# A four-layer convolutional sequence on one core: layer 1's edges reordered, layer 3's preparation with full-width products and a split in two parts

## The chip, the cores and the metric

The kernel runs on one core of a Trainium2 chip. A core has TensorE (PE, matrix products into the accumulator memory PSUM), VectorE (DVE), ScalarE (ACT), GpSimd (POOL) and SyncE (SP, which here only issues transfers). Each engine has an instruction queue of its own, worked through in order; transfers (DMAs) are issued from such a queue and run beside it. The metric is the time of one launch on the device in microseconds (us).

## The reference

Four layers on x of shape (4, 128, 64, 64), float32. In the kernel an image is a tile of 128 partitions (channels) by N = 4096 pixels. The change touches layers 1 and 3.

Layer 0 is an attention with 1x1 products. Layer 1 applies twice a 3x3 convolution with weights rounded to powers of two, and after it an "adder" convolution, then batch norm:

```python
def per_channel(wc):
    return -jnp.sum(jnp.abs(p - wc[None, :, None]), axis=1)
...
out = adder_conv(shift_conv(x, w_shift1, stride=1), w_add1)
out = jax.nn.relu(batchnorm(out, bn1_gamma, bn1_beta))
out = adder_conv(shift_conv(out, w_shift2, stride=1), w_add2)
out = batchnorm(out, bn2_gamma, bn2_beta)
return jax.nn.relu(out + residual)
```

Here p are the 3x3 patches: for each of 128 output channels and each pixel, 1152 absolute differences are summed. The batch norm takes mean and variance over all four images. Layer 2 is an attention with an MLP. Layer 3 splits x by two small maps, projects, and runs a selective scan forwards and backwards over the 4096 pixels:

```python
m = jax.nn.sigmoid(jnp.einsum('bchw,oc->bohw', cat, illum_w[:, :, 0, 0]) + illum_b[None, :, None, None])
f_low = x * m
f_high = x * (1.0 + alpha * curr_grad)
hidden = _rms_norm(seq, rms_w)
xz = jnp.einsum('blc,ec->bel', hidden, in_proj_w)
xs, z = jnp.split(xz, 2, axis=1)
xs = _causal_conv1d(xs, conv_w[:, 0, :], conv_b)
...
delta = jax.nn.softplus(jnp.einsum('brl,dr->bdl', dt, dt_proj_w) + dt_proj_b[None, :, None])
...
return f_mamba + gamma * f_low
```

seq is f_high with its pixels in a row, cat is x with the illumination map as a 129th channel, and both maps have one value per pixel for all channels.

## The kernel before

The program is one pass over the layers; between layers images lie in DRAM (x1d, y1d, y2d) or, in layers 2 and 3, in four image tiles in SBUF (xp[0] to xp[3]). Most instructions are written through a helper that keeps the written order on each engine, so the order of the text is the order of each queue.

**Layer 1.** `layer1` (L535) loads and rounds the weights of both convolutions first: `quantized` (L282) loads one set (L287) and `quantize` (L259) rounds it in nine DVE operations; this is done for both before anything else. `shift_adder` (L292) is then called once for each adder, with the prefix a1 or a2 in the tiles' names. At its start it loads the adder's weights wa (L306), makes negated columns wn (L311) for ACT's biases and a masked copy w_third (L327 to L329), and computes wsum, the sums of wa over input channels, with 192 small matmuls (L335) into the PSUM tile pw, copied at L339. Then it convolves image 0: `fetch` loads rows of the input with a border (xin), nine matmuls (L375) for each of eight blocks of 512 pixels fill a PSUM bank, and DVE copies it into the padded image pb (L380).

The main part walks over 512 units (4 images x 128 output channels). A unit is built from several 128x4096 tiles: absolute values on ACT (L456), maxima on DVE (L470), one of both (L462), and the tiles of `pair` (L474): for each half of the image two maxima on DVE (L479), which a POOL DMA adds into one tile (L481). Each tile is summed over channels by matmuls with a `pick` of 31 zero columns and one non-zero (L425) into PSUM. The order of these steps is written out by hand in a table (ORDER, L43 to L48), for four units at a time; its entries C take three steps of the generator `beside` (L404), which holds the sums of the present image's patches (L387 to L402) and the convolution of the next image. After every 32 units `evacuate` (L432) adds the sums and writes a chunk: L437 and bn_stats L440 on DVE, then the stores to y_d (L442). The four chunks of an image are 32 output channels each.

`batchnorm_scale` (L541) stores all statistics to DRAM (stats_d, L543), reads them back with the channels in the partitions (byco, four DMAs, L546), aggregates them (L550), and takes Ln, Exp and a product (L553) for the scale. The second adder's convolution normalizes its input as it fetches it (`normed`, L571 to L575). After the second adder, `residual` of layer 2 (L660) loads x<-y2d (L671) and applies the scale (L673, L676, L677).

**Layer 3.** `layer3_prepare` (L1004) runs its images one after the other. PSUM has eight banks of 128x512 here, all with the tag mm. The steps:

- `split(b)` (L1042): for each of eight blocks of 512 pixels it loads a row of both maps (mr, L1051), multiplies x by the illumination weights (pm, L1053), adds the illumination row by a product with one row (L1054), and spreads the gradient row by another product with one row (pg, L1056). ACT takes the sigmoid (sg, L1058); DVE makes f_high (fh, L1059) and gamma·f_low (L1061), which is stored (low_d, L1062).
- `norm(b)` (L1064): the RMS norm of fh: squares on ACT, the mean by a product (pv, L1074), Ln and Exp, the scaling on DVE (L1081).
- `project(b)` (L1084): in four pieces of 2048 pixels: px (L1099) copied by ACT (pre, L1100), a causal convolution of four DVE operations per piece (L1122, L1124), pz (L1106) with Silu on ACT (sz, L1108) and its store (L1109), Silu of the convolved piece (xs, L1127) and its store (L1129).
- `steps_of(b)` (L1131): pxd (L1143), copied by DVE (xd, L1146), pd (L1155), dv (L1158), and the softplus over ee and uu on DVE and ACT (L1160 to L1175), a POOL product (L1177), with stores of 1024 columns (delta_d, du_d).

The loop at L1196 runs split(0), norm(0); then for each image project(b), split(b+1), and steps_of(b) with norm(b+1) beside it, one step of norm for two of steps_of. `layer3_scan` (L1215) follows; it reads low_d back and adds a bias in an Identity activation (L1455).

Of the kernel before, what the change touches and what calls it, by code (L numbers as in the profile page):

```python
# [9 lines left out]
F32 = mybir.dt.float32  # L10
# [251 lines left out]
def quantize(nc, sb, w, of, name):  # L262

    flat = [P, TAPS * P]
    aw = sb.tile(flat, F32, tag="qa", name=f"{name}_aw")
    nc.vector.tensor_scalar(aw.bitcast(I32), w.bitcast(I32), 0x7FFFFFFF, None, ALU.bitwise_and)

    pw = sb.tile(flat, F32, tag="qp", name=f"{name}_pw")
    nc.vector.tensor_scalar(pw.bitcast(I32), w.bitcast(I32), 0x7F800000, None, ALU.bitwise_and)
    up = sb.tile(flat, F32, tag="qu", name=f"{name}_up")  # L270
    nc.vector.scalar_tensor_tensor(up, pw, 1.4142135381698608, aw, ALU.mult, ALU.is_lt)
    nc.vector.scalar_tensor_tensor(pw, up, 1.0, pw, ALU.add, ALU.mult)
    nc.vector.scalar_tensor_tensor(pw, aw, 0.005, pw, ALU.is_ge, ALU.mult)
    sg = sb.tile(flat, I32, tag="qu", name=f"{name}_sg")
    nc.vector.tensor_scalar(sg, w.bitcast(I32), -0x80000000, None, ALU.bitwise_and)
    nc.vector.tensor_tensor(pw.bitcast(I32), pw.bitcast(I32), sg, ALU.bitwise_or)
    nc.vector.tensor_tensor(pw, pw, w, ALU.subtract)
    nc.vector.tensor_tensor(of, w, pw, ALU.add)


def quantized(tc, pool, w_shift, tag):

    nc = tc.nc
    wqs = pool.tile([P, TAPS, P], F32, name=f"{tag}wq")
    with tc.tile_pool(name=f"{tag}q", bufs=1) as qp:
        ws = qp.tile([P, TAPS * P], F32, name=f"{tag}ws")
        nc.sync.dma_start(ws, w_shift)  # L287
        quantize(nc, qp, ws, wqs.rearrange("p t o -> p (t o)"), tag)
    return wqs


def shift_adder(tc, cm, load, wqs, w_add, stats, y_d, tag):  # L292
# [10 lines left out]
    with ExitStack() as ctx:  # L303
        cp = ctx.enter_context(tc.tile_pool(name=f"{tag}c", bufs=1))
        wa = cp.tile([P, TAPS, P], F32, name=f"{tag}wa")
        nc.sync.dma_start(wa.rearrange("p t o -> p (t o)"), w_add)  # L306
        wn = {}
        for t, scale in [(t, 1.0) for t in ABS_TAPS[0]] + [(ABS_TAPS[c][i], 0.5) for c, i in HALF.items()]:
            if (t, scale) not in wn:
                wn[t, scale] = cp.tile([P, P], F32, name=f"{tag}wn{t}_{len(wn)}")  # L310
                nc.vector.tensor_scalar(wn[t, scale], wa[:, t, :], -scale, None, ALU.mult)  # L311

        pick = {}
        for v in (-1.0, -2.0):
            pick[v] = cp.tile([P, 63], F32, name=f"{tag}pick{int(-v)}")
            nc.vector.memset(pick[v], 0.0)
            nc.vector.memset(pick[v][:, 31:32], v)
        third = cp.tile([P, 32], F32, name=f"{tag}third")
        nc.vector.memset(third, 0.0)
        nc.vector.memset(third[:, 2:32:4], 1.0)  # L320
# [5 lines left out]
        with tc.tile_pool(name=f"{tag}w", bufs=1) as wt:  # L326
            w_third = wt.tile([P, P], F32, name=f"{tag}wthird")  # L327
            nc.vector.memset(w_third, 0.0)
            nc.vector.tensor_copy(w_third[:, 2:P:4], wa[:, MAX_TAPS[3], 2:P:4])  # L329
            pw = ps_c.tile([P, NC], F32, tag="cv", name=f"{tag}pw")  # L330
            for c in range(NC):
                for g in range(4):
                    for i, t in enumerate(sum_taps):
                        w = w_third if t == MAX_TAPS[3] else wa[:, t, :]
                        nc.tensor.matmul(  # L335
                            pw[32 * g : 32 * g + 32, c : c + 1], w[:, 32 * c : 32 * c + 32], cm.one_col,
                            start=(i == 0), stop=(i == len(sum_taps) - 1), skip_group_check=True,
                        )
            nc.vector.tensor_copy(wsum, pw)  # L339
# [64 lines left out]
        def beside(b, pb_of):  # L404

            yield from sums_of_p(b, pb_of[b], sp_of[b])
            if b < B - 1:
# [4 lines left out]
        for _ in convolution(0, pb_of[0]):  # L412
            pass
# [19 lines left out]
        def evacuate(chunk):  # L433
            b, c = divmod(chunk, NC)
            for k in range(2):
# [6 lines left out]
                nc.sync.dma_start(to[k], o)  # L442

# [29 lines left out]
        def pair(n, h):  # L473
# [7 lines left out]
            then(nc.gpsimd.dma_start(ms[1], ms[0], accum_op=ALU.add))  # L481
# [53 lines left out]
def layer1(ctx, tc, cm, w_shift1, w_add1, g1, b1, w_shift2, w_add2, g2, b2, x1d, y1d, y2d, stats_d):  # L535
# [5 lines left out]
    def batchnorm_scale(stats, at, gamma, name):  # L541

        nc.sync.dma_start(at, stats.rearrange("p c s v -> p c (s v)"))  # L543
        byco = lp.tile([P, 4, 2 * B * 6], F32, name=f"byco{name}")
        for c in range(4):
            nc.sync.dma_start(  # L546
                byco[32 * c : 32 * c + 32], at[:, c, :].rearrange("(g j) s -> j g s", g=4)
            )
# [11 lines left out]
    wq1, wq2 = quantized(tc, lp, w_shift1, "a1"), quantized(tc, lp, w_shift2, "a2")  # L560
# [6 lines left out]
    shift_adder(tc, cm, plain, wq1, w_add1, stats1, y1d, "a1")  # L567
    mean1, sc1 = batchnorm_scale(stats1, stats_d[0], vec["g1"], "1")
# [11 lines left out]
    shift_adder(tc, cm, normed, wq2, w_add2, stats2, y2d, "a2")  # L580
    mean2, sc2 = batchnorm_scale(stats2, stats_d[1], vec["g2"], "2")
# [422 lines left out]
def layer3_prepare(  # L1004
    tc, cm, xp, maps_d, illum_w, illum_wl, illum_b, rms_w, in_w, conv_w, conv_b, x_w, dt_w, dt_b,
    alpha, gamma, low_d, xs_d, sz_d, delta_d, du_d, xdbl_d,
# [3 lines left out]
    with ExitStack() as ctx:  # L1010
# [14 lines left out]
        ga = load([P, 1], gamma.partition_broadcast(P), "ga")  # L1025
# [4 lines left out]
        xw = load([P, 2, NX], x_w, "xw")  # L1030
        dtw = load([DT_RANK, 2 * P], dt_w, "dtw")
# [3 lines left out]
        iwr = cp.tile([1, P], F32, name="iwr")  # L1035
        nc.vector.tensor_scalar(iwr, cm.ones[0:1, :], iwl, None, ALU.mult)
        alr = cp.tile([1, P], F32, name="alr")
        nc.vector.tensor_scalar(alr, cm.ones[0:1, :], al, None, ALU.mult)
# [3 lines left out]
        def split(b):  # L1042

            fh = big.tile([P, N], F32, tag="fh", name=f"fh{b}")
            fh_of[b] = fh
            for k in range(NB):
                u = f"{b}_{k}"
                c = bass.ts(k, BK)
                src = inner(xp, b, k)
                mr = sb.tile([1, 2, BK], F32, tag="mr", name=f"mr{u}")  # L1050
                nc.sync.dma_start(mr, maps_d[:, b, c].rearrange("(o i) n -> o i n", o=1))  # L1051
                pm = ps.tile([P, BK], F32, tag="mm", name=f"pm3_{u}")
                then(nc.tensor.matmul(pm, iwm, src, start=True, stop=False))  # L1053
                then(nc.tensor.matmul(pm, iwr, mr[:, 0, :], start=False, stop=True))  # L1054
                pg = ps.tile([P, BK], F32, tag="mm", name=f"pg{u}")
                then(nc.tensor.matmul(pg, alr, mr[:, 1, :], start=True, stop=True))  # L1056
                sg = sb.tile([P, BK], F32, tag="sg", name=f"sg{u}")
                then(nc.scalar.activation(sg, pm, AF.Sigmoid, bias=ib))  # L1058
                then(nc.vector.scalar_tensor_tensor(rows(fh[:, c]), rows(pg), 1.0, src, ALU.add, ALU.mult))  # L1059
                yield  # L1060
                then(nc.vector.scalar_tensor_tensor(rows(sg), src, ga, rows(sg), ALU.mult, ALU.mult))  # L1061
# [653 lines left out]
```

## Time and profile before

| what | us |
|---|---|
| median of three runs (lowest to highest) | 21133.91 (21114.99 to 21178.35) |
| the profiled execution's own time | 21155.93 |
| its span | 21154.1 |
| PE busy | 19660.1 |
| DVE busy | 18970.2 |
| ACT busy | 17550.0 |
| POOL busy | 7577.3 |

By stage, in the profiled execution (us from the start of the span):

| stretch | what |
|---|---|
| 0 to 1980 | layer 0 |
| 1980 to 2090 | layer 1's weights and the first convolution of image 0 |
| 2090 to 9400 | first adder |
| 9400 to 9504 | its end, statistics, and image 0's second convolution |
| 9504 to 16850 | second adder |
| 16850 to 17880 | its end, and layer 2 |
| 17880 to about 18540 | layer 3's preparation |
| about 18540 to 21154 | layer 3's scan |

Busy times are sums of instruction durations on an engine. A chain of waits is followed back from the last instruction to what released each step, so its pieces lie one after the other in time; a piece named DMA is the time from a transfer's issue to its landing. A float32 matmul of 512 columns appears as two records. The granted PE clock is a share of the full clock.

### The profile page before, as it was taken

What the parts mean: (1) busy time and instruction counts of PE and PEld (TensorE: products, weight loads), DVE (VectorE), ACT (ScalarE), POOL (GpSimd) and SP (SyncE); (2) the same over time, 40 slices, a digit from 0 to 9 for tenths busy, and PEclk for the clock granted to TensorE, in tenths of its full rate; (3) what the DMA queues carried; (4) which work ended last, traced back from release to release, by engine and by line L of the source; (5) the groups of instructions that cost most, each with busy time, mean ns of one, the idle gap of its engine ahead of it and who ended that gap; (6) DMA issues with size and microseconds to landing.
All of it is one profiled execution on the core that took longest, in us unless ns stands there. A gap on an engine that the chain in (4) does not pass through costs nothing.

```text
span 21154.1 us, 323001 instructions
## 1 busy us (share of the span) xinstructions
PE 19660.1 (93%) x139180; PEld 6292.0 (30%) x139180; DVE 18970.2 (90%) x12273; ACT 17550.0 (83%) x9055; POOL 7577.3 (36%) x3844
## 2 busy tenths in 40 slices
PE   9998999999999999999999999999999877789998
PEld 4443222222222222222222222222222223223333
DVE  7876999999999999989999999999999887799998
ACT  5664999999999999989999999999999833466666
POOL 5665222222222222212222222222222100189998
PEclk9999999999999999999999999999999988699999
DMA  0000777777777777767777777777777710389997
GB/s 13 9 9 20 147 152 148 147 154 149 151 145 152 150 143 151 156 136 145 150 148 152 149 148 151 147 149 147 147 154 153 162 21 20 130 238 251 253 253 218
DMA packets 576191, 2970.17 MB, mean 140 GB/s; under 512 B 164572, under 2 KB 165476, under 8 KB 240804
## 3 DMA queue, kind: packets, MB, share of 16 engines
q0 software_dynamic: 296800, 2160.20, 51.0%
q1 hardware_dynamic: 277812, 787.19, 13.0%
q8 instruction: 1089, 17.84, 0.3%
q14 instruction: 346, 2.83, 0.0%
q10 hardware_dynamic: 144, 2.10, 0.0%
HBM read 662.03 MB, written 128.78 MB: 37 GB/s over the span
## 4 chain that ended last, share of the span: by engine, by line
PE 43%; issue 15%; DMA 14%; DVE 14%; ACT 11%; POOL 3%; SPq 1%; DVEq 0%; POOLq 0%; ACTq 0%
PE a1pa L425 15%; PE a2pa L425 13%; DMA ma<-ma 10%; ACT aa L456 9%; PE pe L164 4%; PE pav L207 4%; DVE h L1364 4%; DVE ma L479 3%; DVE da L470 2%; DMA du<-du_d 2%; DVE g L854 1%; POOL ma L481 1%; PE mg L1379 1%; DMA dl<-delta_d 1%; PE a1pc L375 1%
## 5 line engine op out<-in xcount | busy, mean ns | idle before, releaser
L481 POOL DMA_DIRECT2D ma<-ma x2048 | 3799.7, 1870 | 10892.9 <-DVE ma L479 7671.8
L456 ACT ACTIVATE aa<-a1pb,a1wn 128x4096 f32<-128x4096 f32 x1920 | 6959.4, 3711 | 485.5 <-PE a1pa L425 342.0
L456 ACT ACTIVATE aa<-a2pb,a2wn 128x4096 f32<-128x4096 f32 x1920 | 6964.9, 3712 | 358.9 <-PE a2pa L425 340.4
L425 PE MATMUL a1pa<-aa,a1pick 128*32 128x512 f32 x30720 | 3616.8, 600 | 84.4 <-ACT aa L456 81.3
L425 PE MATMUL a2pa<-aa,a2pick 128*32 128x512 f32 x30720 | 3617.2, 600 | 82.6 <-ACT aa L456 81.3
L470 DVE TENSOR_SCALAR da<-a2pb,a2wa 128x4096 f32<-128x4096 f32 x1408 | 3271.0, 2350 | 316.1 <-PE a2pa L425 316.1
L470 DVE TENSOR_SCALAR da<-a1pb,a1wa 128x4096 f32<-128x4096 f32 x1408 | 3269.6, 2350 | 306.8 <-PE a1pa L425 306.5
L425 PE MATMUL a1pa<-da,a1pick 128*32 128x512 f32 x22528 | 2696.1, 597 | 15.2 <-DVE da L470 15.2
L425 PE MATMUL a2pa<-da,a2pick 128*32 128x512 f32 x22528 | 2680.8, 594 | 18.0 <-DVE da L470 18.0
L479 DVE TENSOR_SCALAR ma<-a1pb,a1wa 128x2048 f32<-128x2048 f32 x2048 | 2529.8, 1282 | 71.1 <-DMA ma<-ma 71.1
L479 DVE TENSOR_SCALAR ma<-a2pb,a2wa 128x2048 f32<-128x2048 f32 x2048 | 2530.6, 1282 | 63.5 <-DMA ma<-ma 63.3
L1379 PE MATMUL mg<-h,ident 128*128 128x512 f32 x4096 | 1955.8, 615 | 214.6 <-ACT m L1388 174.0
L1364 DVE TENSOR_TENSOR_SCAN h<-da,h,dbu 128x1024 f32<-128x1024 f32 x768 | 1804.3, 2349 | 126.1 <-ACT da L1350 32.2
L425 PEld LDWEIGHTS a1pa<-aa,a1pick 128*32 128x32 f32 x30720 | 982.4, 111 | 2492.5 <-issue 2130.5
L425 PEld LDWEIGHTS a2pa<-aa,a2pick 128*32 128x32 f32 x30720 | 983.1, 111 | 2488.0 <-issue 2132.9
L425 PE MATMUL a2pa<-ma,a2pick 128*32 128x512 f32 x8192 | 1094.2, 607 | 266.0 <-DMA ma<-ma 265.8
L425 PE MATMUL a1pa<-ma,a1pick 128*32 128x512 f32 x8192 | 1096.2, 608 | 239.1 <-DMA ma<-ma 239.1
L201 POOL TENSOR_TENSOR ssum<-ssum,et 128x512 f32<-128x512 f32 x960 | 1230.0, 1281 | 233.0 <-ACT et L196 166.1
L425 PEld LDWEIGHTS a1pa<-da,a1pick 128*32 128x32 f32 x22528 | 716.9, 110 | 1747.2 <-issue 1612.4
L425 PEld LDWEIGHTS a2pa<-da,a2pick 128*32 128x32 f32 x22528 | 714.8, 110 | 1739.7 <-issue 1584.1
L462 DVE SCALAR_TENSOR_TENSOR aa<-a2pb,a2wa,aa 128x4096 f32<-128x4096 f32 x256 | 1147.4, 4482 | 81.8 <-ACT aa L456 81.7
L462 DVE SCALAR_TENSOR_TENSOR aa<-a1pb,a1wa,aa 128x4096 f32<-128x4096 f32 x256 | 1147.4, 4482 | 78.2 <-ACT aa L456 78.0
(295 smaller groups left out, 17707.1 us busy)
## 6 DMA issues: line engine op xcount, KB each, us to landing
ma<-ma POOLq DMA_DIRECT2D x2048, 1024.0 KB, 8.9
dl<-delta_d SPq DMA_DIRECT2D x256, 512.0 KB
dl<-delta_d SPq DMA_DIRECT2D x512, 256.0 KB
du<-du_d SPq DMA_DIRECT2D x256, 512.0 KB
du<-du_d SPq DMA_DIRECT2D x512, 256.0 KB
sz_d<-sz SPq DMA_DIRECT2D x64, 256.0 KB
xs_d<-xs SPq DMA_DIRECT2D x8, 2048.0 KB
delta_d<-dv SPq DMA_DIRECT2D x32, 512.0 KB
```

Of the source, the lines that this page charges most:

```text
L164: nc.tensor.matmul(pe, k[:, bass.ts(j, P)], unit[u, "q"], start=True, stop=True)
L201: nc.gpsimd.tensor_tensor(unit[u, "sum"], unit[u, "sum"], at, ALU.add)
L207: nc.tensor.matmul(unit[u, "av"], image[u // NB][2][:, j, :], at, start=(j == 0), stop=(j == NJ - 1))
L375: then(nc.tensor.matmul(pc, wqs[:, t, :], here[:, y : y + RB, x : x + W], start=(t == 0), stop=(t == TAPS - 1),))
L425: then(nc.tensor.matmul(pa[k][32 * g : 32 * g + 32, :], pick[v][:, 31 - jj : 63 - jj], d[:, bass.ts(4 * at + g, BK)], start=(n // 32, k) n ...
L456: then(nc.scalar.activation(rows(at), view(n, t), AF.Abs, bias=bias, scale=scale))
L462: then(nc.vector.scalar_tensor_tensor(rows(at), view(n, ADDED_TAP), weight(n, ADDED_TAP), rows(at), ALU.max, ALU.add))
L470: then(nc.vector.tensor_scalar(rows(dt), view(n, t), weight(n, t), None, ALU.max))
L479: then(nc.vector.tensor_scalar(rows(mt), v, weight(n, t), None, ALU.max))
L481: then(nc.gpsimd.dma_start(ms[1], ms[0], accum_op=ALU.add))
L1364: then(nc.vector.tensor_tensor_scan(t[:, cols][:, s], da[:, s], st[n, "dbu", h][:, cols][:, s], 0.0 if e % 4 == 0 else st["last"], ALU.mul ...
L1379: then(nc.tensor.matmul(pm, cm.ident, st[n, way, h][:, bass.ts(k, BK)], start=(way == 0), stop=(way == 1)))
```

## The change

In layer 1:

- Only the first convolution's weights are rounded before it. The second's are loaded behind the first input rows, and their nine DVE operations stand between the copies of image 0's convolution, as do wn and w_third; wa's load is moved there too. The rounding's temporaries take tiles of the maxima's tag "am".
- The 192 small matmuls for wsum become eight further steps of `beside` for image 0, after the sums of patches and ahead of image 1's convolution.
- The memsets of pick and third go from DVE to POOL.
- For the last unit, `pair` issues no accumulating DMA: both maxima are summed by matmuls of their own.
- Statistics don't go through DRAM: at each evacuation of the last image, four DMAs copy the chunk's statistics from SBUF to byco in SBUF; in the last chunk two of them are issued on ACT's queue.

In layer 3:

- The one-row and eight-row operands (map rows, iwr, alr, dtw) and the 40-column one (xw) are padded with zeros to 128, so that each product is 128 by 128. Each map row is loaded by a DMA of its own into the first row of a padded tile, two tiles for each map.
- `split` is divided. `high(b)` has the pg products and fh; for b ≥ 1, fh is written into the buffer of xp[b-1]. `low(b)` has the pm products into eight PSUM banks, eight sigmoids into tiles of the tags dv, ee and uu, four POOL products of 1024 columns, and four stores.
- high(b+1) runs beside project(b), two steps per piece; low(b+1) follows at its end. For image 0 the order is high, norm, low.
- The factor gamma is no longer in f_low; the scan's Identity activation applies it as its scale.

In the compiled order, some small ACT and DVE operations for the scan's constants also stand earlier, in the last image's projection and steps, with four more loads of ACT's function tables.

The diff, cut to its core:

```diff
-def quantized(tc, pool, w_shift, tag):
...
+def quantize(tc, pool, w_shift, of, name):
+    w, aw, pw, up = [
+        pool.tile([P, HL], F32, tag="am", name=f"{name}_q{k}")[:, 0 : TAPS * P] for k in range(4)
+    ]
+    nc.sync.dma_start(w, w_shift)
+    yield
...
-            nc.vector.memset(pick[v], 0.0)
-            nc.vector.memset(pick[v][:, 31:32], v)
+            nc.gpsimd.memset(pick[v], 0.0)
+            nc.gpsimd.memset(pick[v][:, 31:32], v)
...
             yield from sums_of_p(b, pb_of[b], sp_of[b])
+            if b == 0:
+                yield from sums_of_w(w_third)
             if b < B - 1:
...
-        for _ in convolution(0, pb_of[0]):
-            pass
+        quantizing = [quantize(tc, mp, w, of, f"{tag}{k}") for k, (w, of) in enumerate(shifts)]
+        for q in quantizing[:1]:
+            for _ in q:
+                pass
+        for at, _ in enumerate(convolution(0, pb_of[0])):
+            if at == 0:
+                nc.sync.dma_start(wa.rearrange("p t o -> p (t o)"), w_add)
+                for q in quantizing[1:]:
+                    next(q)
+            if at % TAPS == 4 and at > 2 * TAPS:
+                for q in quantizing[1:]:
+                    next(q, None)
+            if at == 2 * TAPS + 1:
+                negated()
...
+            if b == B - 1:
+                for g in range(4):
+                    (nc.scalar if c == NC - 1 and g % 2 else nc.sync).dma_start(
+                        byco[32 * c : 32 * c + 32, g, :],
+                        stats[32 * g : 32 * g + 32, c, :, :].rearrange("p s v -> p (s v)"),
+                    )
...
-            then(nc.gpsimd.dma_start(ms[1], ms[0], accum_op=ALU.add))
+            if n < B * P - 1:
+                then(nc.gpsimd.dma_start(ms[1], ms[0], accum_op=ALU.add))
+            else:
+                streams[n, "q", h] = (-2.0, ms[0], (h,))
             streams[n, "p", h] = (-2.0, ms[1], (h,))
...
-        nc.sync.dma_start(at, stats.rearrange("p c s v -> p c (s v)"))
-        byco = lp.tile([P, 4, 2 * B * 6], F32, name=f"byco{name}")
-        for c in range(4):
-            nc.sync.dma_start(
-                byco[32 * c : 32 * c + 32], at[:, c, :].rearrange("(g j) s -> j g s", g=4)
-            )
...
+        map_rows = [[padded([P, BK], f"map{i}_{j}") for j in range(2)] for i in range(2)]
+        def map_row(i, b, k):
+            t = map_rows[i][k % 2]
+            nc.sync.dma_start(t[0:1, :], maps_d[i, b, bass.ts(k, BK)].rearrange("(o n) -> o n", o=1))
+            return t
...
-        def split(b):
+        def low(b):
+            halves = []
+            for k in range(NB):
+                pm = ps.tile([P, BK], F32, tag="mm", name=f"pm3_{b}_{k}")
+                then(nc.tensor.matmul(pm, iwm, inner(xp, b, k), start=True, stop=False))
+                then(nc.tensor.matmul(pm, iwr, map_row(0, b, k), start=False, stop=True))
+                halves.append(pm)
+            yield
+            for k2, tag in enumerate(("dv", "ee", "uu", "dv")):
+                sg = sb.tile([P, 2 * BK], F32, tag=tag, bufs=3, name=f"sg{b}_{k2}")
+                for i in range(2):
+                    then(nc.scalar.activation(sg[:, bass.ts(i, BK)], halves[2 * k2 + i], AF.Sigmoid, bias=ib))
+                src = xp[b][:, 2 * RB * k2 : 2 * RB * (k2 + 1), :].rearrange("p h w -> p (h w)")
+                then(nc.gpsimd.tensor_tensor(sg, src, sg, ALU.mult))
+                nc.sync.dma_start(low_d[b, :, bass.ts(k2, 2 * BK)], sg)
+        def high(b):
+            if b == 0:
+                fh = big.tile([P, N], F32, tag="fh", name="fh0")
+            else:
+                fh = xp[b - 1].rearrange("p h w -> p (h w)")
...
+                pg = ps.tile([P, BK], F32, tag="mm", name=f"pg{b}_{k}")
+                then(nc.tensor.matmul(pg, alr, map_row(1, b, k), start=True, stop=True))
                 yield
...
                 if i + 1 < len(pieces):
                     projected(*pieces[i + 1])
+                next(beside, None)
+                next(beside, None)
...
+                if i + 1 == len(pieces):
+                    next(beside, None)
+                    next(behind, None)
                 then(nc.scalar.activation(xc, xc, AF.Silu, bias=cb[:, mc : mc + 1]))
...
+            next(behind, None)
...
-            project(b)
-            if b < B - 1:
-                for _ in split(b + 1):
-                    pass
+            more = b < B - 1
+            project(b, high(b + 1) if more else iter(()), low(b + 1) if more else iter(()))
...
-            then(nc.scalar.activation(fl, fl, AF.Identity, bias=lb))
+            then(nc.scalar.activation(fl, fl, AF.Identity, scale=ga, bias=lb))
```

## The prediction, before the result was known

> **What bounds the kernel now.** I read the page's 40 slices first, then busy time by stage, then the chain of waits at each stage's edge. By stage (columns: stretch, its length, busy PE, weight loads, DVE, ACT, POOL, granted PE clock, DMA share, GB/s):
>
> ```profile
> 1980.00:2090.00 110.00, 72.69 (x336) 35.88 (x336) 27.18 (x42) 0.00 (x0) 1.50 (x12) 0.77 0.19 48
> 2090.00:9400.00 7310.00, 6978.05 (x62196) 2043.13 (x62200) 6852.77 (x3804) 6960.73 (x1921) 1874.26 (x1059) 0.98 0.74 150
> 17886.00:17932.00 46.00, 45.63 (x48) 13.30 (x48) 10.18 (x17) 7.63 (x10) 0.00 (x0) 0.50 0.15 48
> 17947.00:17974.00 27.00, 27.00 (x65) 11.93 (x64) 23.93 (x17) 20.40 (x32) 0.00 (x0) 1.00 0.32 126
> ```
>
> Layer 1's two main stretches hold 94 to 95% on PE, ACT and DVE at once, 14,660 us in all: no step added there is quite free. What the change can shorten lies between them. Edge A is 110 us in which ACT does nothing. The third row is one image's split in layer 3: PE is full, but at half clock (0.50); the projection beside it (fourth row) runs at 1.00.
>
> The chain at edge A (start, length, what):
>
> ```profile
> 1980.56 3.76 DMA a1ws<-in_w_shift
> ...
> 1994.89 3.60 DMA a2ws<-in_w_shift
> ...
> 2009.07 3.66 DMA a1wa<-in_w_add
> 2012.76 0.91 DVE a1wn L311 x6
> ...
> 2013.82 7.17 PE a1pw L335 x182
> 2021.00 3.77 DMA a1xin<-x1d
> ```
>
> Between the end of the first quantizing (1994.89) and the first convolution product (2025.02) lie 30.1 us of serial work that this convolution doesn't use. After the first adder and after the second:
>
> ```profile
> 9406.08 7.09 DMA ma<-ma
> ...
> 9417.28 7.26 DMA a2wa<-in_w_add
> ```
>
> ```profile
> 16841.48 7.04 DMA ma<-ma
> ...
> 16852.18 11.66 DMA stats_d<-stats
> ```
>
> In both the last unit's accumulating DMA is 7 us with nothing beside it. Then the statistics travel through DRAM: after the second, 11.66 us before SP may issue the reads, and the first x load of layer 2 stands behind them on SP (issued 16869.77, used 16878.51).
>
> [...]the split is busy 45.63 of 46 us and still at 0.50. Of its three products a block two have one row of 128 (L1054, L1056)[...].[...] The smallest load here takes 2.1 us (iw, 17883.90 to 17885.98).[...] Here DVE L1168 takes 3.25 us (at 18092.58) beside a POOL product, 1.23 without.
>
> **Layer 1, part by part.** Edge A: the second quantizing (3.60 + 10.5), wa's load (3.66), six wn and the third (1.0), the 192 small products (8.0) and the last load (3.8) leave the path. The second quantizing and wn move to DVE inside the first convolution, where PE has 64.9 us and DVE 8 copies of 0.7: they hide; uncovered they would be 11.5 us. Both moved loads, w_shift2 and wa, queue on SP behind the three xin loads already issued, so the convolution's start isn't held. Start about 1995.5 in place of 2025.0: −29.5. The small products run in the main stretch of image 0: 8 us where PE has 5% free; bounds 0 and +8 (an addition can't gain), I take +4. They also push the next image's convolution by 8 of the 93 steps of 3 products, which still ends before the image does. Edge A: −25.
>
> Edge B: the last unit's two maxima go straight to PE, 16 more matmul records; the pairs' 8 records took 1.97 cold, so +1 to +2 for −7.1: statistics ready about 8.3 sooner (9408.5). They go SBUF to SBUF, each chunk's four pieces at its own evacuation, so three quarters are sent long before. The last four DMAs are split over SP and ACT (0.4 each); landing isn't in this trace: bounds 2.1 (iw) and 7.3 (wa, under load); I take 2.5, byco there at about 9411. In before bn_aggr started at 9426.16 and the convolution 12.3 later, held mostly by PE's small products (9424.65 to 9432.8), behind which the xin load was issued (9432.85). Without these: aggregate 1.0, Ln with its 1.28 table and Exp 2.0, multiply 0.2, normalize and relu 1.4 make 4.5; start about 9415.4 in place of 9438.45: −23, +4 for the small products in the main stretch. Edge B: −19.
>
> Edge C: the pair's −8 again. The 11.66 is no longer on SP ahead of x: after the last stores (about 16844) SP has the four reads, some 14 weight loads at 0.43 each and then x, issued about 16853; it took 8.7 from issue to use (16869.77 to 16878.51), so the first DVE pass comes at 16862[...]. The scale is ready before either. In all −12.5 to −17, the pair included; I take −14. Layer 1: −25 −19 −14 = −58.
>
> **Layer 3, part by part.** Each image's split is 24 products. In before:
>
> ```profile
> 17886.37 2.04 PE pm L1053 x2
> 17888.41 2.00 PE pm L1054 x2
> ...
> 17947.06 6.87 PE px L1099 x16
> ```
>
> A product (two records) takes 2.0 cold and 6.87/8 = 0.86 warm. Padding to 128 rows adds no length: L1053 with 128 rows and L1054 with one take the same. If padded rows count as work, 8 blocks × 3 × 0.86 = 20.6 in place of 45.7. That zeros in the moving rows count isn't shown; products with zero weights (the 128*32 pick) run at 0.98, so I take full clock, with half clock as the other bound.
>
> Start: high(0) (8 × 0.86), norm(0), low(0) (16 × 0.86 = 13.7) bring the first px about 23 sooner (17924); but the first convolution now stands behind high(1)'s first DVE step, +5. −17.5.
>
> Per image of the first three: DVE's last convolution ends 17985.1 and its first xd copy is at 18021.61, a gap of 36.5 which the split's half-clock products fill. After: eight fh steps on DVE (8 × 0.69 = 5.5), and waits for PSUM banks, since all eight are in use: px of the second next piece needs high's bank, free after the convolution (2 × 2.2 = 4.4), and low's fourth product needs the bank of the last pg; from there five pairs at 1.72 and two pxd at 1.72 come to about 11.7. Together 21.6 for 36.5: −15. The steps' other PE work (pxd, pd, pv at 0.72 clock, 66.6 busy of 86) speeds up: −4. Four POOL products of 2.6 beside DVE[...]: +2. −17 × 3 = −51. f_low's factor gamma goes into an activation that the scan already has (L1455): nothing. Low's sigmoids are the same eight. The low stores become four of 512 KB; the tags dv, ee, uu they borrow have three buffers each, and steps(b) waits for a store only if it takes over 6 us; I take 0, bound +3 per image.
>
> Last image: the scan's constants move ahead with four more table loads (4 × 1.28 = 5.1 on ACT): +4, its steps' clock −3: about 0. Eight zeroing memsets on POOL run under layer 2's end: 0.
>
> The map rows: 64 loads of one row in place of 32 of two, on SP, two buffers per map. A load waits for the product that frees its buffer and then takes 2.1; two products later is 2.57 (3 × 0.86) in low, more in high, so it just fits. Uncovered it costs 0.5 to 2 each. Behind it on SP stand sz_d, xs_d and low_d stores, and ACT waits for sz buffers already (46 us in the trace). Bounds 0 and +2 per load; I take 0, and see below. Layer 3: −17.5 −51 = −68.
>
> **Sum.** −58 −68 = −126. The profiled run took 21155.9 (span 21154.1), 22.0 over the median 21133.9; 21133.9 − 126 = 21008.
>
> **Rivals.** (1) Padded rows don't raise the clock: low is 27 in place of 13.7, +13 per image and +13 at the start, so layer 3 gives about −17: −75, 21059. For it: nothing shows zeros in moving rows. Against: zeros in weights don't slow.
>
> (2) Gains of layer 3 hidden: between the projection and the steps DVE, SP or PSUM takes the place of PE (ACT's wait for sz_d, 8 banks), and only layer 1's edges remain, partly eaten by the main stretch: −50, 21084. For it: DVE is busy 62.70 of 86 in the steps and 23.93 of 27 in the projection.
>
> (3) Slower: SP's queue. Every one of the 64 map loads waits on SP for its product, and each wait holds all stores behind it, hence sz, ACT's Silu and, through PSUM, PE. It turns the sum at 126/64 = 2 us exposed per row; at 3 to 4 us, which is a load's latency seen in full plus a store's issue, +65 to +130: 21200. For it: SP already holds mr's loads in order (0.54 per issue). Against: two buffers, and half of the loads are issued while DVE's convolutions take 8.4 per piece.
>
> (4) All of it comes without stalls: low hides wholly under the last convolution, steps at clock 1.0: −165, 20969.
>
> **Chances.** Forecast (−126 ± 35) 0.52; rival 1 0.13; rival 2 0.17; rival 3 0.08; rival 4 0.10. A measurement here tells 0.3%, 63 us. Faster by more (below 21070.5): 0.52 + 0.10 + most of rival 1 + a little of 2 = 0.72; same 0.19; slower 0.09. Leaving out rival 3 and the tails: 20935 to 21095.
>
> **What would show it.** Edge A's first a1pc at about 1995; no accumulate at the end of either adder; edge B's first a2pc about 9415 − 29 + 4 = 9390; main stretches 4 longer each; x's first pass 12 to 17 sooner against the adder's end. In layer 3 PEclk near 1.0 in low and high, pg and pm at 0.86 per product, DVE's gap before the first xd near 21, 136 per image in place of 153. I would be wrong if the main stretches grew by over 20, if pm stayed at 2.0, or if ACT's wait for sz_d grew past 60.

## The result, and the profile after

The changed kernel takes 21195.71 us (median of 13 runs, 21185.99 to 21232.45) against 21146.3 for the kernel before beside it: a ratio of 1.0028 with a 95% interval of 1.002 to 1.0035, so 0.28% slower. The forecast was 21008. The profiled execution has a span of 21191.4, 37.3 more than the one of before.

By stage the two traces differ like this. The edges are taken from the last sum of an absolute tile to the first product of what follows.

| stretch | before, us | after, us | difference | forecast |
|---|---|---|---|---|
| start of the span to the first sum of adder 1 (edge A) | 2094.6 | 2064.0 | −30.5 | −29.5 |
| adder 1, first to last sum of an absolute tile | 7310.0 | 7383.5 | +73.5 | +4 |
| from there to the first sum of adder 2 (edge B) | 103.5 | 88.1 | −15.4 | −23 |
| adder 2, the same | 7331.9 | 7419.5 | +87.5 | +4 |
| from there to layer 2's first pass over x (edge C) | 38.6 | 32.1 | −6.5 | −14 |
| layer 2 | 1007.5 | 1007.2 | −0.3 | 0 |
| layer 3's preparation, first scaling of weights to first scan | 657.6 | 591.0 | −66.6 | −68 |
| layer 3's scan to the end | 2610.5 | 2606.2 | −4.3 | 0 |

All that the change was forecast to shorten got shorter, by 124 us together where 134 were forecast (−126 with the +8 in the main stretches). What turned the sign is the two main stretches: +161 in place of +8. (Each column is one execution. Where the code of a stretch is the same, two traces can differ by some 40 us: adder 1 takes 7310.0 us here and 7271.7 in the trace of e6 below, whose layer 1 is that of before.)

The changed kernel by stage (stretch, its length, busy PE, weight loads, DVE, ACT, POOL, granted PE clock, DMA share, GB/s):

```profile
1980.00:2060.00 80.00, 63.72 (x144) 27.77 (x144) 26.55 (x33) 0.00 (x0) 1.84 (x19) 0.88 0.27 65
2060.00:9447.00 7387.00, 6978.37 (x62416) 2051.42 (x62420) 6854.13 (x3805) 6960.28 (x1920) 1928.48 (x1058) 0.98 0.74 148
18022.00:18037.00 15.00, 13.65 (x32) 5.58 (x32) 1.51 (x3) 7.83 (x12) 7.03 (x3) 1.00 0.17 71
18041.00:18066.00 25.00, 24.02 (x57) 10.24 (x56) 19.53 (x16) 14.19 (x21) 0.59 (x1) 1.00 0.25 96
18316.00:18453.00 137.00, 98.56 (x193) 40.29 (x192) 101.75 (x92) 71.66 (x96) 29.94 (x12) 0.84 0.35 142
```

In the second row PE, DVE and ACT were busy no longer than before (6978, 6854 and 6960 us there, 6978, 6853 and 6961 before): the stretch grew by waiting, not by work. The third row is the first image's low: the granted clock is 1.00 there, where it was 0.50 for the split's products in the trace of before. In it every second product is a full one of 128 rows. The padded ones alone are seen in high(0), where PE comes from a pause of 7.5 us:

```profile
17998.79 6.33 PE L1103 MATMUL pg<-map,alr 128*128 128x512 f32 x8 [7.45 <-DMA dtw<-in_dt_proj_w]
18005.69 1.98 PE L1103 MATMUL pg<-map,alr 128*128 128x512 f32 x4 [0.58 <-DMA map<-maps_d]
```

The clock granted there is 0.50 until 18004.12 and 1.00 from then on, after 5.3 us in which PE had done nothing but padded products. The last row of the table above is one whole image of layer 3, 137 us in place of 153.

The chain that ended last can't be followed back through these stages in the trace of after, so the edges are read from the timeline. PE's first product of the first convolution, and DVE's last statistics and aggregate after each adder (start, length, engine, line, form, and in brackets the idle time before and what ended it):

```profile
1995.66 4.91 PE L372 MATMUL a1pc<-a1xin,wq 128*128 128x512 f32 x7 [21.29 <-issue]
...
9453.26 0.69 DVE L454 BATCH_NORM_STATS2 stats<-a1ev 128x6 f32<-128x512 f32 x1
9462.49 1.02 DVE L568 BATCH_NORM_AGGREGATE mv<-byco 128x2 f32<-128x192 f32 x1 [8.54 <-DMA byco<-stats]
...
16960.77 0.69 DVE L454 BATCH_NORM_STATS2 stats<-a2ev 128x6 f32<-128x512 f32 x1
16977.94 1.02 DVE L568 BATCH_NORM_AGGREGATE mv<-byco 128x2 f32<-128x192 f32 x1 [16.48 <-DMA pww<-in_pos_w]
16987.08 2.41 DVE L693 TENSOR_SCALAR x<-x,mv,sc 128x4096 f32<-128x4096 f32 x1 [5.10 <-DMA x<-y2d]
```

The first product of edge A comes as forecast (1995.5) to 0.2 us. At the other two the statistics come later than forecast: 8.5 and 16.5 us from the last statistics to the aggregate, where 2.5 had been put in. At edge B all four copies are issued within 0.7 us of the statistics, and their last packets end at 9461.64, 0.1 us after the last packet of the chunk's own stores, which were issued just ahead of them. At edge C only the two copies on SP's queue go out at once. The two on ACT's queue are issued 12.9 us after the statistics:

```profile
16962.16 1.23 SPq L460 DMA_DIRECT2D byco<-stats  x2
16974.38 1.17 ACTq L460 DMA_DIRECT2D byco<-stats  x2
```

Ahead of them ACT's queue has issued the residual's 2 MB load (16959.98), and then it waits until 16974.34 for the semaphore that the second of SP's copies raises when it has landed (the first of ACT's copies uses the same one). So that copy took 11.5 us, and the two on ACT's queue no more than 3.6.

In layer 3 the first image's pm, and DVE between the last fh step and the first xd copy:

```profile
18087.58 1.02 PE L1083 MATMUL pm<-map,iwr 128*128 128x512 f32 x2
18088.44 1.02 PE L1082 MATMUL pm<-x,iwm 128*128 128x512 f32 x2
18092.89 2.08 PE L1083 MATMUL pm<-map,iwr 128*128 128x512 f32 x2 [3.43 <-DMA map<-maps_d]
...
18084.29 0.68 DVE L1105 SCALAR_TENSOR_TENSOR x<-pg,x 128x512 f32<-128x512 f32 x1
18099.15 0.69 DVE L1197 COPY xd<-pxd 128x512 f32<-128x512 f32 x1 [14.18 <-PE pxd L1194]
```

A pair of records follows the last at 0.86 us, except that one load of a map row comes 3.43 us late. DVE's gap is 14.2 and with the eight fh steps (8 × 0.69) 19.7, where 21.6 was forecast and 36.5 stood before.

**Where the 161 us arise.** Cut by chunks of 32 units, image 0 grew by 34, 30, 10 and 17 us in adder 1 and by 25, 35, 11 and 24 in adder 2. Images 1 to 3 together changed by −17 and −8. Cut finer, by ACT's instructions (15 absolute tiles are one group of four units), adder 1 shows a period:

| group | 8 | 9 | 10 | 11 | 12 | 13 | 14 | 15 | 16 | 17 | 18 | 19 |
|---|---|---|---|---|---|---|---|---|---|---|---|---|
| before, us | 59.3 | 58.8 | 54.4 | 59.6 | 54.4 | 54.4 | 61.6 | 54.4 | 54.4 | 58.8 | 54.4 | 54.4 |
| after, us | 54.4 | 57.4 | 69.1 | 54.4 | 54.4 | 68.9 | 54.4 | 54.4 | 68.8 | 59.3 | 54.4 | 68.0 |

Every third group costs some 14 us more, and some groups behind it get 5 to 7 back. One group takes three steps of `beside` (the entry C), and a block of the convolution has nine steps: the period is that of the blocks. What happens in group 10, in the timeline of after (DVE, POOL, PE):

```profile
2677.73 0.69 DVE L377 COPY a1pb<-a1pc 128x512 f32<-128x512 f32 x1 [2.62 <-PE a1pc L372]
...
2715.18 2.35 DVE L491 TENSOR_SCALAR da<-a1pb,a1wa 128x4096 f32<-128x4096 f32 x1
2729.36 2.35 DVE L491 TENSOR_SCALAR da<-a1pb,a1wa 128x4096 f32<-128x4096 f32 x1 [11.83 <-PE a1pa L439]
...
2677.81 0.13 POOL L350 MEMSET a1xin<- 128x20 f32 x1 [2.58 <-issue]
...
2701.97 17.47 POOL L503 DMA_DIRECT2D ma<-ma  x3 [10.69 <-DVE ma L500]
...
2711.76 1.90 PE L439 MATMUL a1pa<-da,a1pick 128*32 128x512 f32 x16
2723.95 1.94 PE L439 MATMUL a1pa<-ma,a1pick 128*32 128x512 f32 x8 [10.28 <-DMA ma<-ma]
```

The same place in the trace of before:

```profile
2727.43 0.70 DVE L380 COPY a1pb<-a1pc 128x512 f32<-128x512 f32 x1
...
2727.64 0.15 POOL L353 MEMSET a1xin<- 128x20 f32 x1
```

Before, neither the copy of a finished block nor the border memset waits: the block's ninth product was the last step of one entry C, and the copy stands in the next one, some 55 us later. The eight new steps are not a multiple of three. After them the ninth product, the copy and the memset stand in the same entry C, and DVE and POOL, which run ahead of PE, wait 2.6 us for it. Some 24 us later POOL begins to issue an accumulating DMA and is held in that one instruction for 15.7 us (2701.97 to 2717.65; a usual issue takes 0.9 to 2.1). It comes free 0.1 us after DVE's row of maxima has ended: DVE breaks off there because it has to wait for PE. PE waits 10.3 us for that DMA, ACT and DVE wait for PE. In image 0 such issues over 14 us are 0 in both adders of before, and 10 and 9 in those of after.

### The profile page after: what moved, and what is told of

Same layout as the page of the kernel before. It is cut to its first block, busy times and chain, and to the rows that moved or that the text cites. A ratio compares the mean times of both kernels' runs of the same rounds, so it can differ in the third digit from the quotient of the medians.

```text
span 21191.4 us, 323123 instructions
## 1 busy us (share of the span) xinstructions
PE 19565.0 (92%) x139212; PEld 6296.1 (30%) x139212; DVE 18943.4 (89%) x12227; ACT 17555.5 (83%) x9059; POOL 7712.6 (36%) x3878
## 3 DMA queue, kind: packets, MB, share of 16 engines
q1 hardware_dynamic: 275540, 786.97, 12.9%
## 5 line engine op out<-in xcount | busy, mean ns | idle before, releaser
L503 POOL DMA_DIRECT2D ma<-ma x2044 | 3895.4, 1922 | 10906.8 <-DVE ma L500 7682.7
```

## The experiments

Each time is given beside the kernel before on the same chip, with the ratio's 95% interval; from chip to chip the kernel before takes 21078.59 to 21146.3 us, so differences are compared and not times.

**e1: six steps for wsum.** Theory P: the phase costs the 161 us. Rival W: the moved work costs them.

```diff
-                    if g % 2:
+                    if g == 3 or (g == 1 and c < 2):
                         yield
```

> The changed kernel, with one edit: the 192 small products of wsum stand in six steps of beside in place of eight, so that the next image's convolution is again in phase with the three steps that one entry C takes. Theory P (phase): with eight steps the copy of each finished block and the border memset stand in the same entry C as the block's last product, so DVE and POOL wait for PE there, and that costs the 161 us by which the two main stretches grew; with six it goes, and the time is 105 to 130 below the kernel before (about 21025). Rival W (work): the growth comes from the small products and moved work as such; the time stays about 50 above the kernel before.

Measured: 21024.39 against 21129.03, ratio 0.9954 (0.9938 to 0.9971). The main stretches take 7302.1 and 7326.9, no longer than before. The work is the same (96 products in the program, of which the trace has two records each), only in six portions: W falls as the cause of the 161 us. In three chunks of image 0 (2615 to 4039), waits in total, number, longest; before, after and e1:

```profile
ACT aa L456 <- PE a1pa L425: 65.6, 28, 6.3
DVE da L470 <- PE a1pa L425: 62.2, 51, 4.9
PE a1pa L425 <- DMA ma<-ma: 40.8, 16, 5.3
```

```profile
ACT aa L477 <- PE a1pa L439: 117.7, 22, 14.0
DVE da L491 <- PE a1pa L439: 101.7, 30, 11.8
PE a1pa L439 <- DMA ma<-ma: 82.2, 12, 10.3
DVE a1pb L377 <- PE a1pc L372: 18.4, 7, 2.7
POOL a1xin L350 <- issue: 12.9, 5, 2.6
```

```profile
ACT aa L477 <- PE a1pa L439: 61.6, 29, 5.8
DVE da L491 <- PE a1pa L439: 56.2, 47, 4.7
PE a1pa L439 <- DMA ma<-ma: 42.0, 16, 4.8
```

The two waits at the block's end are gone altogether, and with them the long waits for the accumulating DMA in these chunks. A remainder isn't excluded: by ACT's absolute tiles image 0 takes 21 us more than before in each adder of e1 (1846.4 and 1861.6 for 1825.7 and 1840.3), and images 1 to 3 take 29 and 26 less, both within what traces differ by.

**e2 and e5: the kernel before with nothing but empty steps.**

```diff
             yield from sums_of_p(b, pb_of[b], sp_of[b])
+            if b == 0:
+                for _ in range(2):    # e5: range(3)
+                    yield
```

> The kernel before, with two empty steps in beside of image 0 between the sums of patches and the convolution of image 1, in both adders: no work is added, only the phase moves. Theory P: each adder's main stretch grows by 70 to 90, the kernel by 140 to 180. Rival W: no change within 20 us.

> The kernel before, with three empty steps in place of two in beside of image 0: the convolution of image 1 comes later by one more step than with two, but is in phase again with the entries C. Theory P: no change within 20 us, where two empty steps cost 129. If it were the later position and not the phase, it would cost 129 or more.

Measured: two empty steps 21258.34 against 21129.03, 1.0061 (1.0046 to 1.0076); three 21131.29 against 21124.64, 1.0005 (0.9998 to 1.0011). Two steps without any work cost 129 us, somewhat under the 140 expected (in the one trace of each, adder 1 grew by 34 and adder 2 by 91); three cost nothing that these runs can tell. So it is the phase, not the later place and not the work. The waits of e2 are those of after:

```profile
ACT aa L459 <- PE a1pa L428: 99.3, 22, 13.6
PE a1pa L428 <- DMA ma<-ma: 71.7, 11, 10.3
DVE a1pb L380 <- PE a1pc L375: 15.8, 6, 2.6
POOL a1xin L353 <- issue: 11.3, 4, 3.6
```

**e3, e4 and e11: which of the two waits.** In the changed kernel the copy (e3), the fetch with its memset (e4) or both (e11) are written two products later, so that they stand in the next entry C (`copied()` writes the copy that was held back).

```diff
-                then(nc.vector.tensor_copy(pb[:, 1 + RB * k : 1 + RB * (k + 1), 1 : 1 + W], rows(pc)))
+                held.append((k, pc))
+            copied()
...
                 for t in range(TAPS):
+                    if t == 2:
+                        copied()
```

```diff
-                if k < NB - 2:
-                    ahead.append(fetch(b, k + 2))
...
                 for t in range(TAPS):
+                    if t == 2 and k < NB - 2:
+                        ahead.append(fetch(b, k + 2))
```

> The changed kernel with its eight steps, but the DVE copy of a finished block is written two products later, so in image 0 it stands in the next entry C; the border memset on POOL stays where it is. If it is DVE's wait for PE that costs (theory P1), most of the 161 goes: 90 to 125 below the kernel before. If it is POOL's wait with the accumulating DMAs queued behind it (theory P2), the time stays near the changed kernel, 30 to 60 above the kernel before.

> The changed kernel with its eight steps, but the fetch of the block after next (the border memset on POOL and the load on SP) is written two products later; the DVE copy stays where it is. Theory P1 (DVE's wait): the time stays 30 to 60 above the kernel before. Theory P2 (POOL's wait): 90 to 125 below it.

> The changed kernel with its eight steps, and both the DVE copy and the fetch with POOL's memset written two products later. The copy alone took away about 113 of the growth, the memset alone about 33. If the two waits are the whole of it, both together give what six steps gave: 21010 to 21045. If more of the phase matters, it stays above 21060.

Measured: e3 21061.21, 0.997 (0.9957 to 0.9983); e4 21145.24, 1.001 (1.0002 to 1.0019); both against 21129.03. e11 20999.06 against 21078.59, 0.9961 (0.9947 to 0.9975). As differences to the kernel before, −68, +16 and −80, where the change had +49 and six steps −105. Neither of the two pure theories holds: DVE's wait carries most (117 of the 154 between the change and e1), POOL's wait some (33). With both moved the main stretches are 7302.2 and 7328.5, e1's to 2 us, and the −80 and e1's −105 have overlapping intervals. The issues over 14 us in image 0 go with it in part: 10 and 9 in the two adders of the changed kernel and of e4, 5 and 3 in e3, 4 and 4 in e11, 2 and 2 in e1. So e4 gained its 33 without making them fewer; what the memset's wait costs beside them isn't shown. e3 keeps POOL's waits and a few long ones:

```profile
PE a1pa L449 <- DMA ma<-ma: 48.2, 19, 10.3
POOL a1xin L350 <- issue: 12.9, 5, 2.6
```

**e6: layer 3's part alone,** on the kernel before (the hunks of layer 3 in the diff, nothing else).

> The kernel before with layer 3's part of the change alone. The prediction gives -68 for it, the trace of the changed kernel about -67 to -71 (with the scan). If layer 3's gain were lost in part to contention, as in the rival, it would be under 30.

Measured: 21059.49 against 21124.64, 0.9973 (0.9967 to 0.998), −65. The layer's forecast of −68 holds by itself.

**e8: the residual's load behind x,** on top of e1, for edge C.

```diff
-                nc.scalar.dma_start(r, x1d[b])
             nc.sync.dma_start(v, rows(y2d[b]))
+            if own:
+                nc.sync.dma_start(r, x1d[b])
```

> The changed kernel with six steps and, after the second adder, the 2 MB load of the residual behind the load of x on SP's queue, in place of ahead of the statistics' copies on ACT's. In the changed kernel these copies come 16.5 us after the statistics; if the residual's load is what holds them, the aggregate starts 6 to 9 us after the statistics and layer 2 begins 4 to 8 us sooner: 21015 to 21021 where six steps gave 21024. If the copies are slow of themselves, no change.

Measured: 21040.92 against 21124.64, 0.9962 (0.995 to 0.9975), within e1's interval. DVE in the trace of e8:

```profile
16811.65 0.69 DVE L454 BATCH_NORM_STATS2 stats<-a2ev 128x6 f32<-128x512 f32 x1
16820.49 1.02 DVE L568 BATCH_NORM_AGGREGATE mv<-byco 128x2 f32<-128x192 f32 x1 [8.15 <-DMA dww<-in_dw_w]
16833.03 2.41 DVE L694 TENSOR_SCALAR x<-x,mv,sc 128x4096 f32<-128x4096 f32 x1 [6.19 <-DMA x<-y2d]
16837.87 4.49 DVE L697 SCALAR_TENSOR_TENSOR x<-x,bn_b,res 128x4096 f32<-128x4096 f32 x1 [2.43 <-DMA res<-x1d]
```

Half of the expectation came true: the statistics are there after 8.2 us and not 15.8 (e1), so it was the 2 MB load ahead of them on ACT's queue that had held them, and edge C is then like edge B. But x and the residual come one after the other, and from the statistics to the residual's sum it is 26.2 in place of 28.3; layer 2 as a whole gains nothing.

**e7, e9, e10, e12: POOL's held issues.** In the trace of before 94 issues take over 5 us, in that of after 97. All but one in each end 0.1 us after the end of a TENSOR_SCALAR of DVE behind which DVE's row breaks off (its next instruction starts 0.15 us later or more), and within each of them DVE works without a gap, over four to nine instructions. But in the trace of before some 870 issues that begin within one maximum end within the next, which follows without a gap. Why those end so soon and the 94 as a rule only behind the row, the traces don't show. Whether a short operation in DVE's row changes it can be tried: e7 gives DVE a tiny copy behind each pair:

```diff
                 ms.append(mt)
+            if n < P:
+                then(nc.vector.tensor_copy(tiny, bank))    # 128x1, from PSUM; e10: from SBUF
```

e9 is e1 with this line and without `if n < P` (all four images), e12 the kernel before with the same; of the two forecasts for each, the first is for issues that are held in all images, the second for the out-of-phase image alone. The copied value is not used.

> The changed kernel with its eight steps, and in image 0 of each adder one tiny DVE copy from PSUM (128x1) behind each pair of maxima, 256 for each adder; its value is not used. Theory S[...]: a copy from PSUM gives POOL its turn, so the DMA issues over 14 us become fewer than 8 in place of 24 and the time falls by 60 to 120 less the copies' own 15 to 40. Rival: the accumulating DMA is stuck for another reason[...]; the number stays, and the time is 15 to 40 over the changed kernel.

> As the run with 256 tiny copies in image 0 of each adder and eight steps, but the copy reads a column in SBUF and not in PSUM. [...]this copy doesn't help: 15 to 60 above the changed kernel's time, with some 24 DMA issues over 14 us. If it is the short operation, or the pause around it, or that the accumulating DMA waits for one instruction more, it helps as the copy from PSUM did: about 20880.

> The changed kernel with six steps and a tiny copy from PSUM behind every pair of maxima, in all four images of both adders (1024 copies for each adder). With the copies in image 0 alone that image took 55 us for each four units where the others took 56 to 57; [...]the other six images gain 30 to 45 us each: 20610 to 20700. If only the out-of-phase image had the trouble, the copies cost their 0.155 us each on DVE for nothing: 20880 to 21000.

> The kernel before, with the tiny copies from PSUM behind every pair of maxima in all four images and nothing else. [...]each image gains 35 to 65: 290 to 400 below the kernel before. If the effect belongs to the changed kernel's phase, 0 to 80 above it (the copies' own 160 on DVE, in part hidden).

| kernel | us | before beside it | ratio (95%) | main stretches |
|---|---|---|---|---|
| e7, image 0, PSUM | 20881.45 | 21124.64 | 0.989 (0.9875 to 0.9905) | 7227.8, 7258.0 |
| e10, image 0, SBUF | 20858.35 | 21078.59 | 0.9893 (0.9878 to 0.9908) | 7222.1, 7251.7 |
| e9, all images, six steps | 20465.85 | 21078.59 | 0.9708 (0.9693 to 0.9722) | 7031.8, 7042.5 |
| e12, before, all images | 20580.35 | 21078.59 | 0.9762 (0.9747 to 0.9776) | 7026.3, 7037.8 |

e7, e9 and e12 did more than expected, and e10 what its second alternative said. In image 0 of e7, which is still out of phase, no issue is over 7 us, though DVE's 17 us of waits at the blocks' ends are still there. Image 0 takes 1769.6 and 1777.0 us there and 1761.1 and 1763.7 in e9, which is in phase: 9 and 13 us more, where the changed kernel took 72 and 74 more than e1. So the phase does most of its harm through the held issue. In e9 and e12 no issue in the whole execution is over 3 us, where the kernel before had 91 over 8 us. So the kernel before paid for held issues too: with them 498 us go in e12, beside the kernel before on the same chip, about 250 for each adder, which had shown as waits of a few us. (Stretch against stretch it is 284 and 294, but that compares e12 with the trace of before from another chip.) The source of the copy makes no difference that these runs can tell (0.989 from PSUM, 0.9893 from SBUF): e10's first alternative, in which a copy from SBUF doesn't help, falls. The tiny copies take about 0.15 us each; POOL and waits in e9 (the same stretches as above):

```profile
L508 POOL DMA_DIRECT2D ma<-ma x2044 | 3294.5, 1612 | 10798.3 <-DVE a2tiny L506 3891.5
```

```profile
DVE da L495 <- PE a1pa L443: 14.4, 28, 1.1
ACT aa L481 <- PE a1pa L443: 12.5, 12, 1.9
PE a1pa L443 <- DMA ma<-ma: 7.3, 6, 1.7
```

ACT's wait for PE falls from 65.6 in the kernel before to 12.5, and the stretch is bound by ACT's own work: of 7031.8 us it is busy 6957. e9 is the fastest version found, 2.9% under the kernel before. The change, with its small products in six steps, is worth 114 us of that (e12 less e9, both against the same 21078.59).

**e13, e14, e15: is it the operation or the moment.** The tiny copy, in image 0 of the changed kernel, between a pair's two maxima (e13), behind each single maximum (e15), or on POOL itself ahead of the DMA, with DVE's queue untouched (e14: `nc.gpsimd.tensor_copy(tiny, ms[1][:, 0:1])`).

> The changed kernel with eight steps; in image 0 the tiny copy stands between the two maxima of a pair, so that the accumulating DMA doesn't wait for it and two maxima no longer stand back to back, but the maximum ahead of the DMA is followed by the next large operation at once. Theory G[...]: as behind the pair, about 20860 to 20900. Theory B (what counts is the moment at which POOL begins, just behind the pair): 30 to 60 above the changed kernel, issues over 14 us still about 24.

> The changed kernel with eight steps; in image 0 POOL itself copies a column of the pair's tile ahead of the accumulating DMA, DVE's queue is as in the changed kernel. If a later beginning of the DMA is enough (theory B), it helps, to 20850 to 21000. If DVE has to leave a gap (theory G), it doesn't: at or above the changed kernel[...].

> The changed kernel with eight steps; in image 0 the tiny copy stands behind each single maximum of 4096 columns (2.75 a unit) and not behind a pair. Theory G: it helps nearly as much, 20860 to 20950. Theory B: little, 21100 or more.

Measured: e13 20857.57, 0.9884 (0.9869 to 0.9899); e15 20912.34, 0.9912 (0.9895 to 0.9929); e14 20946.9, 0.9927 (0.9912 to 0.9941), all against 21109.05. Longest issue in image 0: 5.6, 11.2 and 4.7 us. Theory G, that a short operation in DVE's row helps wherever it stands, is borne out by e13 and e15, but e14 helps as theory B had it. Four of the five edits in image 0 put a short operation into DVE's row; e14 leaves that row as it is and changes what POOL does and when. A single rule for when an issue ends isn't found, and stays open. What is shown is where the held ones end, that all five edits help, and that the long issues and the time go together; what in the hardware holds them isn't shown.

## Why the prediction was wrong, point by point

- **The step that failed** is the sentence on edge A: the small products "also push the next image's convolution by 8 of the 93 steps of 3 products, which still ends before the image does". It asked only whether the convolution ends in time, not where its blocks' ends come to lie. (A step of the convolution is one product, and an entry C takes three.) Eight is not a multiple of three, and this made DVE wait for PE seven times and POOL five times in image 0 of each adder, for some 2.6 us each, and each such place could bring a held issue of 15.7 us. "8 us where PE has 5% free; bounds 0 and +8" priced the work; e2 shows that the two steps cost 129 us with no work in them. The same holds for edge B's "+4". The work itself was priced well: with the held issues gone, the main stretches of e9 are 5.5 and 4.7 us longer than e12's. The prediction's own sign of being wrong, main stretches that grow by over 20, is the one that came.
- **A cost that the trace of before did show** was not read: 91 issues of POOL over 8 us, and PE's waits for the accumulating DMA. What goes with them, 498 us in all (e12), says that these stretches hang on how long POOL's issues last and not only on three engines at 95%.
- **Edge A** was right: first product at 1995.66 where about 1995 was forecast.
- **Edge B** was 8 short, by the term "landing ... bounds 2.1 (iw) and 7.3 (wa, under load); I take 2.5": the copies took 8.5 from the last statistics, more than the upper bound. That they come behind the chunk's own stores is read from the times of the packets, not tested. **Edge C** was 8 short because two of the copies were issued only when another had landed, with the residual's load ahead of them (e8); the prediction said that "The scale is ready before either", and it was the late one: SP's x load waited until 16979.09, after the aggregate.
- **Layer 3** was right as a sum (−66.6 for −68; alone −65) and nearly so in its parts: 136 us from image to image was forecast, and it was 133.2, 136.3 and 136.8; the start gained 12.6 where 17.5 was forecast. The granted clock went from 0.50 to 1.00 while PE did padded products alone (high(0)), and the low products of the first image ran at 1.00, where the split's had run at 0.50. The half-clock case (rival 1) and the hidden gain (rival 2) didn't come.
- **Map rows**: waits of PE for them are 15.0 us in all in the profile of after, for the pm products. Three of these waits, of 3.4 to 5.1 us, lie in DVE's gap before the first xd copy, where 0 had been put in for them; in the first image the gap's sum held all the same (19.7 for 21.6), so its other terms were too large, and that it fits is in part luck. The rival in which SP's queue loses 2 us at each of 64 loads didn't come; the slower end came by a mechanism that was not among the rivals.

## What to carry to other kernels

When work is put into a generator that a fixed table draws from in portions, ask not only whether it still fits but which instruction now stands beside which: an insertion that isn't a multiple of the portion puts a consumer next to its producer. Test it with empty steps: they cost nothing of themselves (three of them gave a ratio of 1.0005, e5), so what they cost is the phase. And look at the longest durations of a DMA-issuing instruction, not only at its mean (1.87 and 1.92 us here): 91 in before and 93 in after took over 8 us, and the one of 15.7 us shown above kept PE waiting for 10.3, and ACT and DVE with it.

## What the runs showed of the hardware

- Of the 2048 accumulating DMAs that POOL issues in before, 94 took over 5 us to issue, most of them some 9 and seven 15.9, while DVE worked without a gap; 93 of them ended 0.1 us after a maximum behind which DVE's row broke off. One 128x1 copy of about 0.15 us behind each pair on DVE took all of these away, and 498 us of 21078.59 with them (e12).
- While PE ran nothing but products whose moving rows are zero in 127 of 128 rows, after a pause of 7.5 us, the granted clock was 0.50 for 5.3 us (17998.79 to 18004.12) and then 1.00. With such products and full ones in turn it was 1.00, PE busy 13.65 us of 15; in the split of before, two one-row products to each full one, it was 0.50, PE busy 45.63 us of 46.
- The copies of 128 statistics rows from SBUF to SBUF, in four DMAs, could be used 8.2 to 8.5 us after the statistics (e8, edge B of after), hardly less than the 9.4 to the aggregate by way of DRAM at edge B before (9416.77 to 9426.16). With a 2 MB load issued ahead of them one copy took 11.5 us to land.
